# Gates spread by DMA with a later multiply, and the MLPs' inner chunks in groups of four

## The chip, the cores and the metric

The kernel runs on one core of a Trainium2 chip. A core has engines with an instruction stream of their own: TensorE (PE, matrix products), VectorE (DVE), ScalarE (ACT, among other things exp and gelu, whose tables it loads), GpSimd (POOL) and SyncE (SP, which issues most of the transfers here). Each works through its stream in order and waits for others by semaphores. Products land in PSUM, which has eight banks of 128 x 512 floats. The metric is the device time of one execution in microseconds.

## The reference

32 sequences ("batches" below) of 128 tokens with 144 channels pass through four layers, each conditioned by a vector per sequence:

```python
x = _L0_cond_ref(x, ...)  # attention with normed q and k, then gelu(h @ w1 + b1) @ w2 + b2
x = _L1_cond_ref(x, ...)  # a rotation by expm(A) in a subspace of 64
x = _L2_cond_ref(x, ...)  # attention (16 heads of 9), then an MLP with 576 inner channels
x = _L3_cond_ref(x, ...)  # attention, then a mixture of 4 experts, 576 inner channels each
```

In L3 each token weighs its two best experts. Every expert is computed for every token, and multiplied by the token's gate `cw`, which is zero for the two that were not chosen:

```python
cw = jnp.sum(one_hot(topk_idx, NUM_EXPERTS) * gates[..., None], axis=1)
hmid = gelu(einsum('tc,ech->eth', xf, w1) + b1[:, None, :])
eo = einsum('eth,ehc->etc', hmid, w2) + b2[:, None, :]
moe = einsum('te,etc->tc', cw, eo)
```

## The kernel before

**Blocks, groups, ticks.** The kernel treats L0 (with L1 behind it), L2 and L3 as three blocks, `layer` 0, 1, 2 in the code; "second block" is L2 and "third block" is L3. The 32 batches of a block go in eight groups of G = 4. Time is laid out by hand in *ticks*: each tick starts the attention of one batch and works on two older ones, and is cut into named *gaps* in a fixed order: a, e, t, first half of the scores, stats, the weighing of values, o, b0, b, den, pre1, second half of the scores, c, y1, y2, y3, then the row maxima are transposed (nm, L870), z, d, and the attention's projection (L1013) ends the tick. `put(tick, gap, f, ...)` hangs a piece of work in a gap; `put2(tick, gap, to, f, ...)` hangs its first half in one gap and its second in another. Group n of a block starts at tick `t0 = first[layer] + 4 n`, its q and k are made at t0 − 2 and its MLP from t0 + 8 on. The order of calls is the order of each engine's stream: nothing reorders it later.

**PSUM.** `bank` (L82-87) hands out seven of the banks in turn, `ps_m`. A product that takes the next bank waits until the one who used that bank seven takings before has been read out.

**Contraction of 144.** Inputs are kept transposed, 128 channels as the *main* part (hM) and the other 16 with a one for the bias as the *rest* (hR), which stands four times, on each of four tiles of 32 rows (it gets there through a DRAM round trip, hG to hD to hR, L709 and L712). `both` (L717-725) issues the main products of some chunks of 128 outputs and then their rest products, or the other way (`rest_first`), adding up in the same bank. Rest products on different row tiles can run side by side. One fp32 product leaves two rows in the profile.

**q and k.** `qk_chunks` (L753-781) makes q and k of a whole group: three chunks with rests on row tiles 0, 1 and 2, then four ScalarE instructions read the three banks (L766, L774 to L776).

**The MLP of the second block.** 576 inner channels are five chunks of 128, the last half full and called SHARED (index 8 in `hid`). `fc1` (L1020-1038) makes some chunks for all four batches of a group, N = 512, then a small gelu that brings in the table (L1034) and the gelus from PSUM into `hid` (L1037). The rest of chunk m lies on row tile m modulo 3. The group's chunks 0, 1, 2 are made at t0 + 8, and 3 and SHARED at t0 + 9, in gap c, rests first. `mlp2` (through `fc2`, L1040-1044) makes the second layer for one batch: five products into one bank, the last with SHARED. It stands in gaps b and d of t0 + 10 and b and c of t0 + 11.

**The experts of the third block.** The experts are computed in pairs. A pair has nine chunks: four full ones per expert, and one, SHARED, whose halves are the last 64 channels of both. `moe1` (L1166-1168) makes them in three parts of three chunks (part 1 begins with SHARED) at t0 + 8 for pair 0 and t0 + 10 for pair 1, parts 0 and 1, and part 2 one tick later. `moe2_parts` (L1186-1202) makes the second layer of one expert for one batch: four products, which VectorE scales by the gate into `acc`, and, for the pair's even expert, one more product from SHARED, which VectorE adds as it is. For this SHARED must have the gates in it already: `shared_by_gate` (L1171-1180) has POOL spread the pair's gates over 64 columns each (`cwx`), PE transpose the four batches' 128 x 128 (`ps_cw`) and VectorE multiply `hid[:, SHARED]` by the result in PSUM, in gap y1 of the tick that makes SHARED.

Of the kernel before, what the change touches and what calls it, by code (L numbers as in the profile page):

```python
# [12 lines left out]
ALU = mybir.AluOpType  # L13
# [12 lines left out]
SHARED = 8  # L26
NPC = 9
MLP_COLS = NFC * (128 + 128 + C)
PAIR_COLS = NPC * (256 + C)
# [40 lines left out]
def tile_kernel(ctx: ExitStack, tc: tile.TileContext, a: dict, out: bass.AP):  # L70
# [182 lines left out]

    take_nm = ring([128, 128], "nm", 2, fill_nm)
    take_kT = ring([128, 4, G * T], "kT", 2, lambda t: None)
    take_qk = ring([128, 32, SLOT], "qkn", 2, fill_qk)
# [489 lines left out]
    def qk_tiles(g):  # L746
# [4 lines left out]
        return gr[g]["qT"], gr[g]["kT"]  # L751

    def qk_chunks(g):  # L753


        p = PARAMS[g[0]]
        hM, hR = gr[g]["hM_a"], gr[g]["hR_a"]
        qT, kT = qk_tiles(g)
        pss = [bank([128, G * T], f"ps_qk_{g[0]}_{g[1]}_{m}") for m in range(3)]
        cols = [slice(128 * m, 128 * m + 128) for m in range(3)]  # L760
        yield from both(
            [(ps, p.wqk[:, c], hM) for ps, c in zip(pss, cols)],
            [(ps, p.wqkR[rows4(m), cols[m]], hR[rows4(m)]) for m, ps in enumerate(pss)],
            False,
        )
        nc.scalar.copy(qT[:, 0, :], pss[0])  # L766
        if g[0] == 1 and g[1] < 2:
            nc.gpsimd.tensor_copy(kT[:, 3, :], kmask[:, 3:4].to_broadcast([128, G * T]))
        if g == (1, 0):
            for r in (1, 2):  # L770
                nc.scalar.mul(kT[:, r, :], pss[1], kmask[:, r : r + 1])
            gr[g]["k"] = kT, pss[1]
        else:
            nc.scalar.mul(kT[:, 2, :], pss[1], kmask[:, 2:3])  # L774
            nc.scalar.copy(kT[:, 1, :], pss[1])  # L775
        nc.scalar.copy(qT[:, 1, :], pss[2])  # L776
        for j in range(4):
            r = 32 * j + 1
            nc.sync.dma_start(
                kT[r : r + HD, 3, :], qT[r + PITCH : r + PITCH + HD, 1, :]  # L780
            )
# [237 lines left out]

    def fc1(g, p, name, m, to, rest_first):  # L1020


        hM, hR = gr[g]["hM_m"], gr[g]["hR_m"]
        pss = [bank([128, G, T], f"ps_h_{name}_{m + i}") for i in range(len(to))]
        cols = [slice(128 * (m + i), 128 * (m + i) + 128) for i in range(len(to))]
        tiles = [rows4((m + i) % 3) for i in range(len(to))]
        yield from both(
            [(ps, p.w1[:, c], hM) for ps, c in zip(pss, cols)],
            [(ps, p.w1R[r, c], hR[r]) for ps, c, r in zip(pss, cols, tiles)],
            rest_first,  # L1030
        )

        t = small.tile([128, 1], F32, tag="gelu", name=f"gelu_{name}_{m}", bufs=1)
        nc.scalar.activation(t, half, AF.Gelu_apprx_tanh)  # L1034
        for ps, i in zip(pss, to):
            n = 64 if g[0] < 2 and i == SHARED else 128
            nc.scalar.activation(hid[:n, i], ps[:n], AF.Gelu_apprx_tanh)  # L1037
# [8 lines left out]
    def mlp1(g, m, to, rest_first):  # L1046
        return fc1(g, MLPS[g[0]], f"{g[0]}_{g[1]}", m, to, rest_first)

# [65 lines left out]
    def expert_ranks(g):  # L1114


        lg = gr[g]["lg"]
        sh = [128, G, E]
        sh4 = [128, G, E, E]
        cw = small.tile(sh, F32, tag="cw", name=f"cw_{g[1]}", bufs=2)  # L1120
# [45 lines left out]
    def moe1(g, pair, part, rest_first):  # L1166
        to = ((0, 1, 2), (SHARED, 3, 4), (5, 6, 7))[part]
        return fc1(g, PAIRS[pair], f"3_{g[1]}_{pair}", 3 * part, to, rest_first)

    def shared_by_gate(g, pair):  # L1170


        cwx = late.tile([128, G, 2, 64], F32, tag="cwx", name=f"cwx_{g[1]}_{pair}", bufs=1)
        cw = gr[g]["cw"][:, :, 2 * pair : 2 * pair + 2]
        nc.gpsimd.tensor_copy(cwx, cw.unsqueeze(3).to_broadcast([128, G, 2, 64]))
        yield
        ps = bank([128, G, T], f"ps_cw_{g[1]}_{pair}")
        for i in range(G):
            nc.tensor.transpose(ps[:, i, :], cwx[:, i, :, :].rearrange("p e c -> p (e c)"), ident)  # L1179
        nc.vector.tensor_tensor(hid[:, SHARED], hid[:, SHARED], ps, ALU.mult)  # L1180

# [4 lines left out]
    def moe2_parts(g, e, i):  # L1186
# [7 lines left out]
        yield  # L1194
        if e % 2 == 0:
            nc.tensor.matmul(  # L1196
# [3 lines left out]
        nc.vector.scalar_tensor_tensor(acc, ps[:, 0, :], w, acc, ALU.mult, ALU.add)  # L1200
        if e % 2 == 0:
            nc.vector.tensor_tensor(acc, acc, ps[:, 1, :], ALU.add)
# [123 lines left out]
    for layer in range(3):  # L1326
        ahead = 5 if layer == 0 else 6
        for n in range(NG):
# [344 lines left out]
```

## Time and profile before

| what | us |
|---|---|
| median of 3 runs (lowest, highest) | 1279.36 (1277.12, 1282.75) |
| the profiled execution's own time | 1276.88 |
| its span, first to last instruction | 1275.2 |
| PE busy | 1226.3 (96% of the span) |
| DVE busy | 808.1 (63%) |
| ACT busy | 779.4 (61%) |
| POOL busy | 667.9 (52%) |
| inner products of all MLPs, ps_h from hM (L721) | 144.1 for the group of tile mlps |
| table loads for gelu (L1034) | 58 of 1.283 |
| table loads for exp (L934) | 57 of 1.283 |
| transposes of spread gates (L1179) | 64 instructions |

The mean granted clock of PE is 0.989 of full speed. In the trace the second block's attention runs from about 420 us and the third's from about 800 us; the first 420 us hold the first block, the rotation's preparation and loads of weights. A row of a time line gives the start, the time from the start of the first to the end of the last instruction in it, engine, line, operation and tiles, and how many; in brackets stands idle time just before it and who ended it. An engine's starts tell the pitch of its instructions better than their durations, since PE overlaps them.

### The profile page before, as it was taken

The page shows a single profiled execution, that of the slowest core. Times are in us where ns is not written, and L with a number is a line of the kernel's source. Part 1 is how long each engine was busy: PE and PEld are TensorE (multiplying, and loading weights), DVE is VectorE, ACT ScalarE, POOL GpSimd, SP SyncE. Part 2 cuts the span into 40 slices and gives each one's busy share as a digit, 9 for nine tenths or more (in the row PEclk, how much of TensorE's full clock was granted, in tenths as well). Part 3 has the DMA queues.
Part 4 walks back from the last instruction along what each step waited for, and adds up shares of the span by engine and source line. Part 5 has one row for each costly group of instructions (what it writes and reads, how often), then busy time and mean ns, then how long its engine had stood idle before and what let it go on. Part 6 is the DMA issues. An engine that isn't in the chain of part 4 may idle for free.

```text
span 1275.2 us, 35382 instructions
## 1 busy us (share of the span) xinstructions
PE 1226.3 (96%) x13980; PEld 898.6 (70%) x13980; DVE 808.1 (63%) x2540; ACT 779.4 (61%) x1724; POOL 667.9 (52%) x1641
## 2 busy tenths in 40 slices
PE   6889888999989999999999999999999999999998
PEld 4668666778766677767677777767676767677666
DVE  5598888877875466666666766645454646454343
ACT  2467777688776665667666666565656555555431
POOL 5567777766754444444545554626262636261610
PEclk9699999999999999999999999999999999999999
DMA  8301011010013111111121111210101010100000
GB/s 227 75 4 38 3 37 37 2 38 21 20 36 132 56 39 55 35 49 45 41 87 56 56 47 46 85 47 15 51 11 55 11 55 11 55 20 17 20 27 10
DMA packets 50328, 56.49 MB, mean 44 GB/s; under 512 B 4560, under 2 KB 35792, under 8 KB 49904
## 3 DMA queue, kind: packets, MB, share of 16 engines
q1 hardware_dynamic: 49504, 53.75, 14.2%
q8 instruction: 113, 1.85, 0.6%
q10 hardware_dynamic: 656, 0.44, 0.2%
q14 instruction: 55, 0.45, 0.1%
HBM read 39.99 MB, written 13.00 MB: 42 GB/s over the span
## 4 chain that ended last, share of the span: by engine, by line
PE 70%; DVE 4%; ACT 0%; issue 0%; POOL 0%; DVEq 0%
PE ps_h L721 20%; PE ps_f L1191 10%; PE ps_s L918 7%; PE ps_w L918 6%; PE ps_o L949 6%; PE ps_qk L721 5%; PE ps_f L1043 4%; PE ps_pj L1013 3%; PE ps_v L721 3%; PE ps_f L1196 1%; DVE nm L930 1%; PE ps_o L870 1%; PE ps_hT_m L690 1%; PE ps_cw L1179 1%; PE ps_hT_a L690 1%; PE ps_d L1092 0%
## 5 line engine op out<-in xcount | busy, mean ns | idle before, releaser
L930 DVE TENSOR_REDUCE nm<-ps_s 128x4 f32<-128x512 f32 x384 | 246.5, 683 | 95.9 <-PE ps_w L918 74.8
L934 ACT ACTIVATE pr<-ps_w 128x512 f32<-128x512 f32 x384 | 208.5, 595 | 149.7 <-PE ps_w L918 141.0
L918 PE MATMUL ps_s<-kT,qT 32*128 32x256 f32 (+2 forms) x1536 | 235.1, 409 | 0.9 <-ACT kT L850 0.9
L918 PE MATMUL ps_w<-q,kT 32*128 32x128 f32 x3072 | 230.0, 284 | 0.0
L918 PEld LDWEIGHTS ps_w<-q,kT 32*128 32x128 f32 x3072 | 194.4, 187 | 11.0 <-issue 6.2
L1037 ACT ACTIVATE hid<-ps_h 128x512 f32<-128x512 f32 (+1 forms) x224 | 120.4, 590 | 99.8 <-PE ps_h L721 99.4
L918 PEld LDWEIGHTS ps_s<-kT,qT 32*128 32x128 f32 x1536 | 136.9, 187 | 29.4 <-issue 9.2
L721 PE MATMUL ps_h<-hM_m,mlps 128*128 128x512 f32 x304 | 144.1, 607 | 0.0
L1200 DVE SCALAR_TENSOR_TENSOR acc<-ps_f,cw,acc 128x144 f32<-128x144 f32 x128 | 46.7, 365 | 146.3 <-PE ps_f L1191 71.5
L999 POOL TENSOR_TENSOR x_sb<-x_sb,res_a 128x144 f32<-128x144 f32 x96 | 46.9, 489 | 156.5 <-DVE res_a L1002 155.8
L949 PE MATMUL ps_o<-pr,vaug 128*32 128x128 f32 x3072 | 104.4, 277 | 0.0
L949 PEld LDWEIGHTS ps_o<-pr,vaug 128*32 128x32 f32 x3072 | 78.6, 110 | 32.7 <-PE ps_w L918 17.4
L721 PEld LDWEIGHTS ps_h<-hM_m,mlps 128*128 128x128 f32 x304 | 53.4, 190 | 66.9 <-issue 65.6
L1043 PE MATMUL ps_f<-mlps,hid 128*128 128x144 f32 x640 | 93.7, 294 | 0.0
L1043 PEld LDWEIGHTS ps_f<-mlps,hid 128*128 128x128 f32 x640 | 82.4, 191 | 8.8 <-issue 4.7
L934 ACT ACT_TABLE_LOAD x57 | 73.1, 1283 | 10.0 <-PE ps_w L918 9.1
L793 POOL TENSOR_SCALAR kT<-kT,cst 128x512 f32<-128x512 f32 x30 | 46.9, 1562 | 58.5 <-ACT kT L775 57.0
L1034 ACT ACT_TABLE_LOAD x58 | 74.4, 1283 | 1.0
L661 POOL TENSOR_SCALAR rs_m_a<-mv_m_a 128x2 f32<-128x2 f32 x81 | 15.5, 191 | 113.5 <-DVE mv_m_a L659 86.6
L1191 PEld LDWEIGHTS ps_f<-pair,hid 128*128 128x128 f32 x512 | 66.9, 190 | 8.4 <-issue 7.6
L701 ACT ACTIVATE hM_m<-ps_hT_m,modM 128x128 f32<-128x128 f32 x96 | 44.6, 465 | 45.8 <-PE ps_hT_m L690 43.8
L1191 PEld LDWEIGHTS ps_f<-mlps,hid 128*128 128x128 f32 x512 | 66.7, 190 | 7.9 <-issue 6.9
(336 smaller groups left out, 2756.2 us busy)
## 6 DMA issues: line engine op xcount, KB each, us to landing
gates<-gates SPq DMA_DIRECT2D x48, 288.0 KB
hD_m<-hG_m SPq DMA_DIRECT2D x24, 256.0 KB
hR_m<-hD_m SPq DMA_DIRECT2D x24, 256.0 KB
hD_a<-hG_a SPq DMA_DIRECT2D x16, 256.0 KB
hR_a<-hD_a SPq DMA_DIRECT2D x16, 256.0 KB
x_sb<-in_x SPq DMA_DIRECT2D x8, 288.0 KB
out_x<-x_sb SPq DMA_DIRECT2D x7, 288.0 KB
mlps<-in_L_mlp SPq DMA_DIRECT2D x2, 1000.0 KB
```

What stands on the lines that cost most here:

```text
L721: nc.tensor.matmul(ps, x, y, start=k == 0, stop=k == 1)
L793: eng.tensor_scalar(o, k, m, None, ALU.mult)
L918: nc.tensor.matmul(o, x, y, start=True, stop=True)
L930: nc.vector.tensor_reduce(to, view, AX.X, ALU.max, negate=True)
L934: nc.scalar.activation(pr[:, 4 * e : 4 * e + 4, :].rearrange("p s q -> p (s q)"), view, AF.Exp, scale=SCALE,)
L949: nc.tensor.matmul(po[rows4(j), t, :], v[:, 4 * j + 2 * t + r, :], prs[j // 2][:, 4 * (j % 2) + 2 * r + t, :], start=r == 0, stop=r == 1,)
L999: nc.gpsimd.tensor_tensor(x_sb[:, b, :], x_sb[:, b, :], t, ALU.add)
L1034: nc.scalar.activation(t, half, AF.Gelu_apprx_tanh)
L1037: nc.scalar.activation(hid[:n, i], ps[:n], AF.Gelu_apprx_tanh)
L1043: nc.tensor.matmul(ps, hid[:, at0, i, :], w2[:, m, :], start=m == 0, stop=m == NFC - 1)
L1191: nc.tensor.matmul(ps[:, 0, :], hid[:, at0 + m, i, :], w2[:, at0 + m, :], start=m == 0, stop=m == 3)
L1200: nc.vector.scalar_tensor_tensor(acc, ps[:, 0, :], w, acc, ALU.mult, ALU.add)
```

## The change

It has three parts.

1. **Second block.** A group's chunks 0 to 3 are made together at t0 + 8 in gap c, main rows first, with rests on row tiles 0 to 3. The fifth, SHARED, is made with the q and k of the group three later (or of the third block's first groups), at t0 + 10 in gap c, as a fourth chunk of `qk_chunks` with its rest on row tile 3; its gelu comes after the four ScalarE instructions of q and k. `mlp2` of the four batches stands in d of t0 + 10 and b, c and d of t0 + 11.
2. **Third block, pair 1 of groups 0 to 4.** Chunks 0, 1, 2 and 4 at t0 + 10 and 5 to 8 at t0 + 11, rests first, and SHARED (chunk 3) with the q and k of the group three later at t0 + 10. Pair 0 of all groups and pair 1 of groups 5 to 7 keep their three parts.
3. **Gates.** The gates are kept as rows e, i of one 128 x 128 tile (`cwz`); one transpose per group turns it, ScalarE copies 16 rows, one transfer writes them to DRAM, and per pair two transfers spread them over 64 partitions each (`gate_rows`, `gate_rows_of`). VectorE multiplies SHARED by that tile in SBUF a tick later than before, in gap stats. One buffer serves both pairs. The SHARED product of batch 0 of a group moves from the pair's even expert to its odd one.

The packing of the rest weights follows the tiles (`MLP_TILES`).

```diff
+MLP_TILES = {
+    "L0": (0, 1, 2, 0, 1), "L2": (0, 1, 2, 3, 3),
+    "L3_0": (0, 1, 2, 0, 1, 2, 0, 1, 2), "L3_1": (1, 2, 3, 3, 0, 1, 0, 2, 3),
+}
+    take_cw = ring([128, 128], "cwz", 2, zeros)
...
+    JOIN = {(1, n): (1, n - 3) for n in range(3, NG)}
+    JOIN.update({(2, n): (1, n + NG - 3) for n in range(3)})
+    JOIN.update({(2, n): (2, n - 3) for n in range(3, NG)})
...
-        yield from both(
-            [(ps, p.wqk[:, c], hM) for ps, c in zip(pss, cols)],
-            [(ps, p.wqkR[rows4(m), cols[m]], hR[rows4(m)]) for m, ps in enumerate(pss)],
-            False,
-        )
+        main = [(ps, p.wqk[:, c], hM) for ps, c in zip(pss, cols)]
+        rest = [(ps, p.wqkR[rows4(m), cols[m]], hR[rows4(m)]) for m, ps in enumerate(pss)]
+        f = JOIN.get(g)
+        if f is not None:
+            l, mlp, m = ("L2", MLPS[1], 4) if f[0] == 1 else ("L3_1", PAIRS[1], 3)
+            psh, main_h, rest_h = fc1_products(f, l, mlp, f"{f[0]}_{f[1]}_s", (m,))
+            main, rest = main + main_h, rest + rest_h
+        yield from both(main, rest, False)
...
         nc.scalar.copy(qT[:, 1, :], pss[2])
+        if f is not None:
+            gelus(f, f"{f[0]}_{f[1]}_s", psh, m, (SHARED,))
...
-    def fc1(g, p, name, m, to, rest_first):
+    def fc1_products(g, l, p, name, ms):
...
+    def fc1(g, l, p, name, ms, to, rest_first):
+        pss, main, rest = fc1_products(g, l, p, name, ms)
+        yield from both(main, rest, rest_first)
+        gelus(g, name, pss, ms[0], to)
...
-        to = ((0, 1, 2), (SHARED, 3, 4), (5, 6, 7))[part]
-        return fc1(g, PAIRS[pair], f"3_{g[1]}_{pair}", 3 * part, to, rest_first)
+        ms = range(3 * part, 3 * part + 3)
+        if part > 2:
+            ms = ((0, 1, 2, 4), (5, 6, 7, 8))[part - 3]
+        to = [(0, 1, 2, SHARED, 3, 4, 5, 6, 7)[m] for m in ms]
+        return fc1(g, f"L3_{pair}", PAIRS[pair], f"3_{g[1]}_{pair}", ms, to, rest_first)
...
-        cwx = late.tile([128, G, 2, 64], F32, tag="cwx", name=f"cwx_{g[1]}_{pair}", bufs=1)
-        cw = gr[g]["cw"][:, :, 2 * pair : 2 * pair + 2]
-        nc.gpsimd.tensor_copy(cwx, cw.unsqueeze(3).to_broadcast([128, G, 2, 64]))
-        yield
-        ps = bank([128, G, T], f"ps_cw_{g[1]}_{pair}")
-        for i in range(G):
-            nc.tensor.transpose(ps[:, i, :], cwx[:, i, :, :].rearrange("p e c -> p (e c)"), ident)
-        nc.vector.tensor_tensor(hid[:, SHARED], hid[:, SHARED], ps, ALU.mult)
+        ws = gr[g]["cwb"].rearrange("p (i t) -> p i t", i=G)
+        nc.vector.tensor_tensor(hid[:, SHARED], hid[:, SHARED], ws, ALU.mult)
+
+    def gate_rows(g):
+        ps = bank([128, 128], f"ps_cw_{g[1]}")
+        nc.tensor.transpose(ps, gr[g]["cwz"], ident)
+        rows = late.tile([128, T], F32, tag="lgT", name=f"cwT_{g[1]}")[: E * G]
+        nc.scalar.copy(rows, ps[: E * G])
+        gr[g]["cwD"] = dram.tile([E * G * T], F32, name=f"cwD_{g[1]}")
+        nc.sync.dma_start(gr[g]["cwD"].rearrange("(r t) -> r t", t=T), rows)
+        gate_rows_of(g, 0)
+
+    def gate_rows_of(g, pair):
+        ws = gr[g]["cwb"] = late.tile([128, G * T], F32, tag="cwb", name=f"cwb_{g[1]}_{pair}")
+        for e in range(2):
+            at0 = (2 * pair + e) * G * T
+            nc.sync.dma_start(
+                ws[64 * e : 64 * e + 64], gr[g]["cwD"][at0 : at0 + G * T].partition_broadcast(64)
+            )
...
-        if e % 2 == 0:
+        shared = e % 2 == (i == 0)
+        if shared:
...
-                put2(t0 + 8, "c", "c", mlp1, g, 0, (0, 1, 2), True)
-                put2(t0 + 9, "c", "c", mlp1, g, 3, (3, SHARED), True)
+                put2(t0 + 8, "c", "c", mlp1, g, 0, (0, 1, 2, 3), False)
                 for i in range(G):
-                    put(t0 + (10, 10, 11, 11)[i], "bdbc"[i], mlp2, g, i)
+                    put(t0 + (10, 11, 11, 11)[i], "dbcd"[i], mlp2, g, i)
...
+                put(t0 + 8, "den", gate_rows, g)
+                put(t0 + 9, "den", gate_rows_of, g, 1)
...
-                    put2(at_, "stats", "b0", moe1, g, pair, 0, True)
+                    if pair and n < NG - 3:
+                        put2(at_, "stats", "b0", moe1, g, pair, 3, True)
+                        put2(at_ + 1, "stats", "b0", moe1, g, pair, 4, True)
+                    else:
+                        put2(at_, "stats", "b0", moe1, g, pair, 0, True)
...
-                    else:
+                    elif not pair or n >= NG - 3:
                         put2(at_, "den", "pre1", moe1, g, pair, 1, False)
-                    put2(at_ + 1, "stats", "b0", moe1, g, pair, 2, True)
-                    put2(at_, "stats", "y1", shared_by_gate, g, pair)
+                    if not pair or n >= NG - 3:
+                        put2(at_ + 1, "stats", "b0", moe1, g, pair, 2, True)
+                    put(at_ + 1, "stats", shared_by_gate, g, pair)
```

More of the change, by code (lines that the diff above doesn't have):

```diff
@@ L1018, in project_sum, with gelus @@
         residual(b, st[s].pop("pj"), gr[g]["ga"][:, i, :], f"a_{s}", layer == 0)
-    def fc1(g, p, name, m, to, rest_first):
+    def fc1_products(g, l, p, name, ms):
         hM, hR = gr[g]["hM_m"], gr[g]["hR_m"]
[L1024 to L1031, printed above, removed]
+        pss = [bank([128, G, T], f"ps_h_{name}_{m}") for m in ms]
+        cols = [slice(128 * m, 128 * m + 128) for m in ms]
+        tiles = [rows4(MLP_TILES[l][m]) for m in ms]
+        main = [(ps, p.w1[:, c], hM) for ps, c in zip(pss, cols)]
+        rest = [(ps, p.w1R[r, c], hR[r]) for ps, c, r in zip(pss, cols, tiles)]
+        return pss, main, rest
+    def fc1(g, l, p, name, ms, to, rest_first):
+        pss, main, rest = fc1_products(g, l, p, name, ms)
+        yield from both(main, rest, rest_first)
+        gelus(g, name, pss, ms[0], to)
+    def gelus(g, name, pss, m, to):
         t = small.tile([128, 1], F32, tag="gelu", name=f"gelu_{name}_{m}", bufs=1)
@@ L1046, in mlp1 @@
     def mlp1(g, m, to, rest_first):
-        return fc1(g, MLPS[g[0]], f"{g[0]}_{g[1]}", m, to, rest_first)
+        ms = range(m, m + len(to))
+        return fc1(g, ("L0", "L2")[g[0]], MLPS[g[0]], f"{g[0]}_{g[1]}", ms, to, rest_first)
     def mlp2(g, i):
@@ L1119, in expert_ranks @@
         sh4 = [128, G, E, E]
-        cw = small.tile(sh, F32, tag="cw", name=f"cw_{g[1]}", bufs=2)
+        gr[g]["cwz"] = take_cw()
+        cw = gr[g]["cwz"][:, : E * G].rearrange("p (e i) -> p i e", i=G)
         rank = small.tile(sh, F32, tag="rank", name=f"rank_{g[1]}", bufs=2)
@@ L1200, in moe2_parts @@
         nc.vector.scalar_tensor_tensor(acc, ps[:, 0, :], w, acc, ALU.mult, ALU.add)
-        if e % 2 == 0:
+        if shared:
             nc.vector.tensor_tensor(acc, acc, ps[:, 1, :], ALU.add)
@@ L1592, with mlp @@
         arrays[f"{name}_wproj"] = wp
-    def mlp(name, w1, b1, w2):
+    def mlp(name, w1, b1, w2, tiles):
         rest = np.zeros((128, w1.shape[1]), w1.dtype)
         for m in range(w1.shape[1] // 128):
-            k, cols = m % 3, slice(128 * m, 128 * m + 128)
+            k, cols = tiles[m], slice(128 * m, 128 * m + 128)
             rest[32 * k : 32 * k + CR, cols] = w1[CM:, cols]
@@ L1609 @@
         w2 = np.vstack([w2, b2, pad[:63, :1].repeat(C, 1)])
-        mlp(l, np.hstack([w1, pad[:C]]), np.hstack([b1, pad[C]]), w2)
+        mlp(l, np.hstack([w1, pad[:C]]), np.hstack([b1, pad[C]]), w2, MLP_TILES[l])
     for n in range(2):
@@ L1619 @@
         w2 = np.vstack([w2[0][:512], w2[1][:512], w2[0][512:], w2[1][512:]])
-        mlp(f"L3_{n}", w1, b1, w2)
+        mlp(f"L3_{n}", w1, b1, w2, MLP_TILES[f"L3_{n}"])
     arrays["L3_b2"] = inputs["L3_cond_b2"].ravel()
```

## The prediction

> **What bounds the kernel now.** I read the busy time by stage first, since the page's averages mix three blocks. The last five stages cover blocks two and three:
>
> ```profile
> 420.00:570.00 150.00, 149.36 (x1739) 106.56 (x1738) 96.86 (x279) 94.33 (x185) 71.30 (x162) 1.00 0.17 49
> 570.00:800.00 230.00, 227.78 (x2842) 165.28 (x2844) 155.09 (x440) 151.07 (x292) 117.64 (x246) 1.00 0.19 56
> 800.00:1000.00 200.00, 199.96 (x1927) 140.93 (x1919) 107.18 (x330) 115.42 (x214) 96.63 (x207) 1.00 0.12 39
> 1000.00:1180.00 180.00, 179.60 (x1768) 129.94 (x1769) 93.60 (x277) 101.54 (x183) 80.64 (x175) 1.00 0.10 30
> 1180.00:1275.00 95.00, 90.18 (x579) 61.57 (x571) 36.76 (x111) 33.14 (x66) 28.75 (x59) 1.00 0.07 19
> ```
>
> Columns: stretch, length, busy PE, PEld, DVE, ACT, POOL, clock, DMA share, GB/s. PE is busy 757 of 760 us up to 1180 at clock 1.00. Work taken from PE shortens the kernel one to one; a hole in PE's stream lengthens it by as much, unless a later wait shrinks with it, and hardly a wait is left.
>
> Second, the time line of PE where q and k of a group are made, and ScalarE's of the same stretch:
>
> ```profile
> 606.18 2.84 PE L721 MATMUL ps_qk<-hM_a,L_wqk 128*128 128x512 f32 x6
> 608.95 1.13 PE L721 MATMUL ps_qk<-hR_a,L_wqkR 32*128 32x512 f32 x6
> 610.01 0.33 PE L870 MATMUL ps_o<-cst,nm 128*128 128x128 f32 x1
> 610.18 1.39 PE L1043 MATMUL ps_f<-mlps,hid 128*128 128x144 f32 x10
> 611.40 0.27 PE L690 MATMUL ps_hT_m<-cst,xh_m 128*128 128x128 f32 x1
> ```
>
> ```profile
> 610.11 0.58 ACT L766 COPY qT<-ps_qk 128x512 f32<-128x512 f32 x1 [2.64 <-PE ps_qk L721]
> 610.59 0.69 ACT L774 ACTIVATE kT<-ps_qk,cst 128x512 f32<-128x512 f32 x1
> 611.17 0.59 ACT L775 COPY kT<-ps_qk 128x512 f32<-128x512 f32 x1
> 611.63 0.61 ACT L776 COPY qT<-ps_qk 128x512 f32<-128x512 f32 x1
> ```
>
> Three chunks' rest rows cost 610.01 − 608.95 = 1.06 us beside 2.77 of main rows, and a second-layer product follows at a pitch of 1.22/10 = 0.122. ScalarE empties the q and k banks until 612.24, which is 2.23 after the rests end.
>
> Third, ScalarE at an inner layer, the price of a gelu from a cold table:
>
> ```profile
> 587.77 1.28 ACT L1034 ACT_TABLE_LOAD   x1
> 589.07 0.20 ACT L1034 ACTIVATE gelu<-half 128x1 f32<-128x1 f32 x1
> 589.18 1.69 ACT L1037 ACTIVATE hid<-ps_h 128x512 f32<-128x512 f32 x3
> ```
>
> The first real gelu starts 1.41 after its table load and takes 0.59 (mean in the page's groups: 0.590).
>
> **The change, part by part.**
>
> *Slots saved.* Chunks of a rest slot run side by side on 32-row tiles; a fourth tile is free beside three. Block two has 5 chunks in two slots, and gets one own slot (four chunks) and a place in q and k's slot: 8 slots fewer. In block three pair 1 of groups 0 to 4 goes from three slots to two and a place: 5 fewer. 13 × 1.06 = −13.8 us on PE, booked below with the block that each belongs to. That four tiles run together shows in the scores: at 605.07 and 605.09 eight rows of scores on four tiles start as one. [...]
>
> *Gates.* Per pair four transposes go (908.73 to 909.22: 0.49), per group one (0.11) comes. Pair 0: 8 × (0.11 − 0.49) = −3.0. Pair 1 of the three groups that keep their form: −1.5; that of the other five is inside the next part. POOL loses 16 copies, which nobody on PE waited for, and the shared product of a pair's first batch moves to its second expert, 0.24 here or there. New: one ScalarE copy of 128x128 per group (0.45 like hM's), and 40 transfers on SP's queue. The gate rows leave after out_x (872.95, held by POOL), and the multiply is wanted by PE at the shared product, 884.77 in that group. The nearest row for a trip through DRAM:
>
> ```profile
> 872.95 0.39 SPq L1211 DMA_DIRECT2D out_x<-x_sb  x1
> 891.28 0.37 SPq L709 DMA_DIRECT2D hD_a<-hG_a  x1
> 894.99 0.33 SPq L712 DMA_DIRECT2D hR_a<-hD_a  x1
> ```
>
> 3.7 us for the way out, as much for the way back: 873.35 + 3.7 + 0.7 for two issues + 3.7 = 881.5, then 0.68 of multiply: 2.6 us to spare; the queue has nothing behind them until 891.28. The second pair's broadcasts wait on the queue for the first multiply (one buffer), which DVE, idle 881.3 to 885.2, gives in time. Taken: 0, and +1 for the last group, where PE has less other work; bounds −0.5 and +3 per group.
>
> *The joined chunk of block two.* Its gelu stands on ScalarE behind the four copies of q and k, and needs the table. With T the end of the rests: copies to T+2.23, table and start +1.41, gelu +0.59: T+4.2. But fc2 of the group's first batch now stands at "d" of this very tick, behind the maxima's transpose: its fifth product reads that chunk, and PE is there at T + 0.17 + 8 × 0.122 = T+1.15. PE is in order, so everything of the tick behind it (transposes of h, pj, the next scores) waits 3.1 us. Eight groups: +24.8. Bounds: 2.6, if the table were loaded half a microsecond sooner, and 3.6 with a mask or transfer in the way of a copy.
>
> *The group of four in block two.* Before, rests came first and each gelu followed its own main product (589.18 while PE ran to 590.07). Now mains come first, so no bank is whole until the rests run. With the table loaded by then, four gelus follow at a pitch of 0.48 (three take 1.55 at 897.56): banks free at T+0.69, 1.17, 1.65 and 2.13. Seven banks turn in a ring. Counted out from the order of PE, the next tick's first scores get the banks of the third and fourth gelu in groups 0 to 5, and PE wants them at T+1.35 (the maxima, transposes and projection lie between): 2.13 − 1.35 = 0.75 to 0.8 of waiting. In groups 6 and 7 the values' products lie between too: 0.3. 4 × 0.75 + 2 × 0.8 + 2 × 0.3 = +5.2. Bounds: 0 and 8 × 1. The other fc2 products only change places within two ticks; they cost the same.
>
> *Pair 1 of five groups in block three.* Rest rows first, so a fourth bank is taken before the scores' banks are read out:
>
> ```profile
> 892.67 0.59 PE L918 MATMUL ps_s<-kT,qT 32*128 32x384 f32 x2
> 893.64 1.06 PE L721 MATMUL ps_h<-hR_m,mlps 32*128 32x512 f32 x6
> ```
>
> ```profile
> 893.83 1.29 DVE L930 TENSOR_REDUCE nm<-ps_s 128x4 f32<-128x512 f32 x2 [0.69 <-PE ps_w L918]
> ```
>
> The fourth rest row waits for the first reduce, 893.83 + 0.69 = 894.52 against 893.64: +0.9. The other four-chunk slot likewise: +0.85. After q and k the next scores take the bank that the joined gelu frees at T+4.2, wanted at T+2: +2.2. Together 3.95, less about 0.4 because each hole gives DVE time for the next. Against it stand the group's saved slot, 1.06, and its transposes, 0.49: 3.95 − 0.4 − 1.55 = +2.0. Five groups: +10. Bounds: −1.55 each (no wait comes) and +3. Ten more table loads of 1.28 lie in this on ScalarE, which is busy 115 of 200 us.
>
> *Sum.* Block two: 24.8 + 5.2 − 8 × 1.06 = +21.5. Block three: +10 − 3.0 − 1.5 + 1 = +6.5. Together +28 on the profiled execution's 1276.88 us, which lies 2.5 under the median of the runs (1279.36): about 1305.
>
> [...]
>
> **The rivals.**
> - *Everything arrives in time* (the other side: faster). −13.8 − 7.0 (64 transposes less 8) = −21: 1256. It needs the joined gelu within T+1.15 in block two; half way to this is where the stall falls under 1.1 us, as then 8 × 1.06 pays for it. For it: ScalarE is idle half its time. Against it: its own order, copies ahead of the gelu, and 1.41 of table.
> - *Only the stall in block two*: all the bank waits hidden by other waits. 24.8 − 13.8 − 7.0 = +4: 1281.
> - *Gates late*: transfers of 128 KB slower than those above by 3 us past their slack. DVE then holds the multiply and behind it the sums' reads, and PE the shared product: 3 × 8 = 24 more: 1329. Against it: DMA share 0.10 to 0.12 here.
> - *The fourth tile does not run beside three*: each four-tile slot 0.86 longer, like a main chunk (2.77/3 = 0.92 at most). Of 31 such slots (16 in block two, 15 in block three) those before a wait hide it; 13 do not: +11, 1316. Against it: the scores' rows.
>
> **How the numbers follow.** The sum 0.65, in 1290 to 1318; all in time 0.10; only the stall 0.10; gates late 0.08; fourth tile 0.07. Predicted 1305. The range 1280 to 1322 leaves out the first rival, the gates' and the tails: 0.2. What a measurement tells from no change is about 0.5%, 6.4 us: faster 0.10, same 0.09 (most of the second rival), slower 0.81.
>
> **What the profile of the changed kernel would show.** Right: at ps_f behind ps_qk in block two a hole on PE of about 3 us ended by the gelu, eight times; holes of under 1 us at the scores behind the group of four, ended by ScalarE; in block three holes at ps_h's rests ended by DVE and at scores ended by ScalarE; PE's share some 2% lower; ps_cw at 8 transposes. Rest slots of eight rows at about 1.1 us. Wrong: the gelu of the joined chunk before the copies, a hole ended by a DMA at the shared product, or a clock under 1.00 after holes, which no row here prices.

## The result: 70 us slower, more than twice the loss that was forecast

The changed kernel takes 1351.18 us (median of 6 runs, 1345.42 to 1357.08) against 1281.03 us for the kernel before (6 runs, 1277.12 to 1284.04). The ratio is 1.0555, its 95% interval 1.0516 to 1.0593. The forecast was 1305, range 1280 to 1322: the direction was right and the size was not. The profiled execution has a span of 1351.4 us.

The stages of the second and third block in the profile after (columns as before: stretch, length, busy PE, PEld, DVE, ACT, POOL, clock, DMA share, GB/s):

```profile
420.00:570.00 150.00, 144.53 (x1602) 103.32 (x1603) 88.17 (x256) 86.72 (x170) 66.84 (x150) 0.97 0.15 44
570.00:800.00 230.00, 202.09 (x2384) 147.37 (x2378) 131.94 (x372) 127.66 (x243) 97.64 (x206) 0.94 0.15 47
800.00:1000.00 200.00, 187.66 (x1891) 133.26 (x1888) 104.75 (x316) 118.31 (x217) 90.34 (x187) 0.97 0.15 48
1000.00:1180.00 180.00, 176.55 (x1606) 122.03 (x1604) 89.33 (x262) 104.08 (x184) 84.52 (x174) 0.96 0.12 39
1180.00:1351.00 171.00, 164.68 (x1313) 115.69 (x1313) 77.09 (x230) 76.74 (x145) 55.00 (x117) 1.00 0.11 32
```

Two columns have changed: PE now has idle time in every stage, and the clock, which was 1.00 in all five, lies between 0.94 and 1.00. Both must be read. For all kernels of this study I split PE's time from 420 us to its last instruction into three: idle time between its rows, half of the time it worked at a granted clock of one half (what that cost), and the rest. The rest is the work at full clock; waits too short to show as a gap between two rows are still in it. All three are worked out from PE's rows and the clock's rows of the profiled executions, to about half a microsecond; a gap counts as idle from 0.15 us.

| kernel (profiled execution, us) | rest | idle | lost to half clock |
|---|---|---|---|
| before | 847.1 | 3.5 | 0 |
| after | 846.9 | 50.3 | 29.3 |

Idle time adds 46.8 and the half clock 29.3, together 76.1, which is what the span grew by (1351.4 − 1275.2 = 76.2). The rest is level, though 56 transposes and 13 slots were removed, some 18 us by the rows (an estimate: 7 and 11). As much was lost again inside rows that the profile calls busy; the places are named below.

Whom PE waited for (engine, line and tile that waited, who ended the wait: us in total, times, the longest), profile after:

```profile
PE ps_f L1060 <- ACT hid L1054: 23.7, 8, 3.0
PE ps_o L884 <- DVE nm L944: 18.9, 15, 2.6
...
PE ps_w L932 <- ACT hid L1054: 4.4, 4, 1.1
PE ps_f L1230 <- DVE hid L1196: 1.9, 1, 1.9
```

The first line is the forecast wait for the joined gelu. The second was not forecast. Before, this wait came to 2.3 us in five places:

```profile
PE ps_o L870 <- DVE nm L930: 2.3, 5, 0.7
```

**The joined gelu.** The tick that makes q, k and the fifth chunk, PE first, then ScalarE:

```profile
582.81 0.33 PE L884 MATMUL ps_o<-cst,nm 128*128 128x128 f32 x1
582.98 1.15 PE L1060 MATMUL ps_f<-mlps,hid 128*128 128x144 f32 x8
587.09 0.85 PE L1060 MATMUL ps_f<-mlps,hid 128*128 128x144 f32 x2 [2.96 <-ACT hid L1054]
...
588.15 1.17 PE L1027 MATMUL ps_pj<-L_wproj,oT 128*128 128x144 f32 x4
```

```profile
584.43 0.61 ACT L788 COPY qT<-ps_qk 128x512 f32<-128x512 f32 x1
585.06 1.28 ACT L1051 ACT_TABLE_LOAD   x1
586.35 0.20 ACT L1051 ACTIVATE gelu_s<-half 128x1 f32<-128x1 f32 x1
586.46 0.57 ACT L1054 ACTIVATE hid<-ps_h_s 64x512 f32<-64x512 f32 x1
```

Eight products of the four chunks that were ready, then a hole of 2.96 until the gelu behind the last copy and the table load is done. The hole has the same length in all eight groups.

**The clock.** Behind this hole the projection's four products take 1.17 us from first start to last end, against 0.66 in the profile before:

```profile
590.83 0.66 PE L1013 MATMUL ps_pj<-L_wproj,oT 128*128 128x144 f32 x4
```

The same stretch of the profile after, in windows of 2 us, shows why:

```profile
584.00:586.00 2.00, 0.13 (x2) 0.00 (x0) 0.00 (x0) 1.98 (x4) 0.00 (x0) 1.00 0.00 0
586.00:588.00 2.00, 0.91 (x4) 0.91 (x5) 0.03 (x1) 1.02 (x3) 0.00 (x0) 0.52 0.08 18
588.00:590.00 2.00, 2.00 (x14) 1.72 (x16) 0.59 (x2) 0.81 (x2) 0.74 (x2) 0.50 0.08 18
...
594.00:596.00 2.00, 2.00 (x32) 1.70 (x31) 1.35 (x4) 0.76 (x3) 1.89 (x5) 1.00 0.22 74
```

The clock falls to one half from 586.1 and comes back at 592.9. Eleven such stretches, of 3.41 or 6.83 us, lie between 420 us and the end of PE's work; the kernel before has none there (the half clock in its first 420 us and behind PE's last row is not counted).

**The maxima.** The tick behind the group of four, where the second slot used to stand, PE's last scores and what follows, then VectorE:

```profile
571.17 0.28 PE L932 MATMUL ps_w<-q,kT 32*128 32x128 f32 x2
572.93 0.30 PE L884 MATMUL ps_o<-cst,nm 128*128 128x128 f32 x1 [1.48 <-DVE nm L944]
```

```profile
571.50 1.28 DVE L944 TENSOR_REDUCE nm<-ps_s 128x4 f32<-128x512 f32 x2
```

PE wants to transpose the row maxima of the scores, and VectorE has only just begun to reduce the second half of them. Before, a slot of two chunks stood at t0 + 9 between the scores and this transpose, 2.78 us (596.60 to 599.38) in which the reduces ran unseen:

```profile
596.60 1.02 PE L721 MATMUL ps_h<-hR_m,mlps 32*128 32x512 f32 x4
597.56 1.99 PE L721 MATMUL ps_h<-hM_m,mlps 128*128 128x512 f32 x4
599.38 0.27 PE L870 MATMUL ps_o<-cst,nm 128*128 128x128 f32 x1
```

The change emptied that place. The hole is 1.48 in groups 0 to 3 and 2.1 to 2.6 in groups 4 to 7.

### The profile page after: what moved, and what is told of

It is laid out like the page before. It is cut to its first block, busy times and chain, and to the rows that moved or that the text cites. A ratio compares the mean times of both kernels' runs of the same rounds, so it can differ in the third digit from the quotient of the medians.

```text
span 1351.4 us, 35333 instructions
## 1 busy us (share of the span) xinstructions
PE 1254.7 (93%) x13924; PEld 915.5 (68%) x13924; DVE 810.5 (60%) x2540; ACT 797.6 (59%) x1742; POOL 667.8 (49%) x1627
## 4 chain that ended last, share of the span: by engine, by line
PE 62%; DVE 6%; ACT 5%; issue 2%; DMA 1%; POOL 0%; SPq 0%; DVEq 0%; ACTq 0%
PE ps_h L726 18%; PE ps_f L1224 8%; PE ps_s L932 6%; PE ps_w L932 6%; PE ps_o L963 5%; PE ps_qk L726 4%; PE ps_f L1060 3%; PE ps_pj L1027 3%; DVE nm L944 2%; PE ps_v L726 2%; ACT L1051 1%; PE ps_f L1230 1%; PE ps_h_s L726 1%; PE ps_o L884 1%; ACT pr L948 1%
## 5 line engine op out<-in xcount | busy, mean ns | idle before, releaser
L932 PE MATMUL ps_w<-q,kT 32*128 32x128 f32 x3072 | 241.5, 291 | 4.4 <-ACT hid L1054 4.4
L932 PE MATMUL ps_s<-kT,qT 32*128 32x256 f32 (+2 forms) x1536 | 241.9, 419 | 0.9 <-ACT kT L864 0.9
L932 PEld LDWEIGHTS ps_w<-q,kT 32*128 32x128 f32 x3072 | 202.7, 193 | 14.6 <-ACT hid L1054 8.2
L932 PEld LDWEIGHTS ps_s<-kT,qT 32*128 32x128 f32 x1536 | 142.0, 192 | 32.7 <-issue 13.2
L1054 ACT ACTIVATE hid<-ps_h 128x512 f32<-128x512 f32 (+1 forms) x211 | 113.7, 594 | 84.8 <-PE ps_h L726 84.7
L1234 DVE SCALAR_TENSOR_TENSOR acc<-ps_f,cwz,acc 128x144 f32<-128x144 f32 x128 | 46.8, 365 | 186.5 <-PE ps_f L1224 97.6
L726 PE MATMUL ps_h<-hM_m,mlps 128*128 128x512 f32 x278 | 132.8, 616 | 0.0
L1060 PE MATMUL ps_f<-mlps,hid 128*128 128x144 f32 x640 | 96.1, 295 | 23.7 <-ACT hid L1054 23.7
L963 PE MATMUL ps_o<-pr,vaug 128*32 128x128 f32 x3072 | 111.1, 288 | 0.0
L963 PEld LDWEIGHTS ps_o<-pr,vaug 128*32 128x32 f32 x3072 | 83.2, 115 | 36.4 <-issue 16.2
L948 ACT ACT_TABLE_LOAD x62 | 79.5, 1283 | 19.7 <-PE ps_w L932 18.9
L1013 POOL TENSOR_TENSOR x_sb<-x_sb,res_m 128x144 f32<-128x144 f32 x64 | 32.8, 514 | 93.8 <-DVE res_m L1016 93.8
```

The lines of the kernel that those rows point to most:

```text
L726: nc.tensor.matmul(ps, x, y, start=k == 0, stop=k == 1)
L932: nc.tensor.matmul(o, x, y, start=True, stop=True)
L948: nc.scalar.activation(pr[:, 4 * e : 4 * e + 4, :].rearrange("p s q -> p (s q)"), view, AF.Exp, scale=SCALE,)
L963: nc.tensor.matmul(po[rows4(j), t, :], v[:, 4 * j + 2 * t + r, :], prs[j // 2][:, 4 * (j % 2) + 2 * r + t, :], start=r == 0, stop=r == 1,)
L1013: nc.gpsimd.tensor_tensor(x_sb[:, b, :], x_sb[:, b, :], t, ALU.add)
L1060: nc.tensor.matmul(ps, hid[:, at0, i, :], w2[:, m, :], start=m == 0, stop=m == NFC - 1)
```

## The experiments

Times are medians. The first four share 13 runs of the kernel before (1277.79), the next four 7 runs (1278.92), the last four 19 (1278.93). The split of each profiled execution:

| kernel | median | ratio to before (95%) | rest | idle | half clock |
|---|---|---|---|---|---|
| gates | 1275.09 | 0.9981 (0.9954 to 1.0009) | 842.9 | 5.2 | 0 |
| l2g | 1331.09 | 1.0411 (1.0385 to 1.0438) | 845.7 | 45.5 | 11.5 |
| l3g | 1295.58 | 1.0112 (1.0075 to 1.0149) | 851.9 | 10.4 | 10.2 |
| fc2_late | 1328.77 | 1.0392 (1.0365 to 1.0418) | 860.9 | 28.9 | 11.9 |
| gelu_first | 1303.43 | 1.0203 (1.0158 to 1.0248) | 843.4 | 22.0 | 8.5 |
| cover | 1306.77 | 1.0202 (1.0155 to 1.0249) | 863.7 | 16.6 | 1.7 |
| cover_rests | 1311.29 | 1.0252 (1.0206 to 1.0299) | 855.9 | 21.6 | 5.1 |
| cover_rests_l2 | 1305.5 | 1.0185 (1.0131 to 1.0239) | 851.9 | 21.8 | 8.3 |
| filler | 1297.1 | 1.0149 (1.0113 to 1.0185) | 866.1 | 7.6 | 0 |
| three_one | 1278.46 | 1.0000 (0.9976 to 1.0024) | 844.9 | 8.8 | 0 |
| three_one_l3 | 1285.14 | 1.0035 (1.0009 to 1.0060) | 848.6 | 8.7 | 1.7 |
| four_rests | 1328.62 | 1.0403 (1.0366 to 1.0441) | 839.0 | 31.1 | 31.5 |

The theory to test was: the loss is holes on PE that the moved chunks open, and the half clock follows from the holes. The rivals: the half clock comes from something else that is new (four-tile slots, transfers), the loss lies mainly in the third block, or the gates' transfers cost.

### The three parts, one by one

`gates` keeps both blocks' chunks as before and has the new gates alone:

```diff
-    JOIN = {(1, n): (1, n - 3) for n in range(3, NG)}
-    JOIN.update({(2, n): (1, n + NG - 3) for n in range(3)})
-    JOIN.update({(2, n): (2, n - 3) for n in range(3, NG)})
+    JOIN = {}
...
-                    if pair and n < NG - 3:
+                    if pair and (2, n + 3) in JOIN:
...
-                put2(t0 + 8, "c", "c", mlp1, g, 0, (0, 1, 2, 3), False)
+                put2(t0 + 8, "c", "c", mlp1, g, 0, (0, 1, 2), True)
+                put2(t0 + 9, "c", "c", mlp1, g, 3, (3, SHARED), True)
                 for i in range(G):
-                    put(t0 + (10, 11, 11, 11)[i], "dbcd"[i], mlp2, g, i)
+                    put(t0 + (10, 10, 11, 11)[i], "bdbc"[i], mlp2, g, i)
```

> Part 3 of the change alone: gates spread by DMA and multiplied a tick later, both blocks' inner chunks as before. Theory (holes on PE and the half clock after them, all from the chunks): 56 transposes fewer, -7 us, and the one wait of 1.9 us at the last group's shared product, so -5: 1276. No half clock beyond the first 420 us. Rival (the transfers and the later multiply hold up the third block): +5 or more: 1286 and waits for a DMA or for hid at ps_f.

`l2g` adds the second block's part to that (its JOIN holds the first two lines), `l3g` the third block's (its JOIN holds {(2, n): (2, n − 3)} alone, and the second block is placed as in `gates`).

> Parts 1 and 3: the second block's chunks as in the change, the third block's pair 1 in three parts as before. Theory: in the second block 8 holes of 2.96 at ps_f (24), 8 at the row maxima (17), some 5 behind the group of four, 18 of half clock, less 7 for the slots: +57, with the gates' -5: 1333. Rival (the third block's joined groups carry most of the loss): below 1310.

> Parts 2 and 3: the second block as before, the third block's pair 1 as in the change. Theory: 5 holes of about 1 after q and k, some 6 of waiting inside the rest rows, 10 of half clock in three places, less 4 for the slots: +16, with the gates' -5: 1292. Rival (the half clock is brought over from the second block's holes and does not arise here): +6 - 5: 1282.

Measured: 1275.09, 1331.09 and 1295.58. Against `gates`, the second block's part costs 56.0 us and the third's 20.5; with the 2.7 that the gates alone lie under before, that makes 73.8, beside the 70.2 measured for the whole. The second block carries the loss, so that rival falls. The gates' transfers do harm in one place alone: at the last group VectorE waits 2.5 us for the spread gates, and PE behind it 2.0 us for the multiplied SHARED:

```profile
DVE hid L1194 <- DMA cwb<-cwD: 2.5, 1, 2.5
```

```profile
PE ps_f L1228 <- DVE hid L1194: 2.0, 1, 2.0
```

In `gates` there is no half clock between 420 us and PE's last row, and its time is not told apart from before. In `l3g` the half clock arises in the third block with no hole in the second, so it is not brought over:

```profile
800.00:1000.00 200.00, 195.97 (x1800) 133.88 (x1796) 99.44 (x300) 119.24 (x213) 94.51 (x198) 0.97 0.15 51
1000.00:1180.00 180.00, 177.91 (x1675) 126.33 (x1668) 94.69 (x285) 101.90 (x184) 81.97 (x172) 0.98 0.11 36
```

### Taking the reader of the late gelu away

```diff
-                    put(t0 + (10, 11, 11, 11)[i], "dbcd"[i], mlp2, g, i)
+                    put(t0 + 11, "bbcd"[i], mlp2, g, i)
```

> The change with one edit: in the second block the four fc2 products of a group all stand at t0 + 11 (b, b, c, d), so none waits for the joined chunk's gelu in its own tick. Theory (the holes are the cause, and the half clock follows from them): the eight holes of 2.96 go, 24, and the half clock behind them, about 11: 1351 - 35 = 1316; the holes at the row maxima stay. Rival (the half clock comes from the four-tile rest slots or the transfers, not from the holes): -24 alone: 1327, with as many stretches at half clock as before. Second rival (the wait moves to the next reader of that bank or to ScalarE's exps): above 1340.

1328.77: 22 less than after, where 35 was expected. The eight holes at ps_f are gone, and the half clock fell from 29.3 to 11.9, but the rest grew by 14. The time line of the same tick shows where the rest grew: the scores of the next tick, whose bank the late gelu still holds, run from 580.79 to the weighing at 583.17, 2.4 us where such scores take 1.1 (595.35 to 596.45 in the same trace). Two of their lines:

```profile
580.79 0.91 PE L932 MATMUL ps_s<-kT,qT 32*128 32x384 f32 x4
581.60 1.08 PE L932 MATMUL ps_w<-q,kT 32*128 32x128 f32 x7
```

So the wait moved in part to the next reader of the bank, inside rows that the profile calls busy. Eight times 1.2 explains 10 of the 14. The second rival was right in kind, not in size. That the first rival had named 1327 is chance: it wanted as many stretches of half clock as before, and they fell from eleven to six.

### The gelu ahead of the copies

The table is loaded before the products, and the gelu is issued before q's and k's four instructions:

```diff
             main, rest = main + main_h, rest + rest_h
+            gelu_table(f"{f[0]}_{f[1]}_s", m)
         yield from both(main, rest, False)
+        if f is not None:
+            gelus(f, f"{f[0]}_{f[1]}_s", psh, m, (SHARED,), False)
         nc.scalar.copy(qT[:, 0, :], pss[0])
...
         nc.scalar.copy(qT[:, 1, :], pss[2])
-        if f is not None:
-            gelus(f, f"{f[0]}_{f[1]}_s", psh, m, (SHARED,))
```

> The change with one edit: where a chunk is joined to q and k, gelu's table is loaded before the products, and the gelu stands ahead of the four ScalarE instructions of q and k. Theory (the holes at ps_f come from the place of that gelu behind the copies and a cold table): the gelu is done about 0.7 after the rests, before PE reaches the fifth product at 1.15, so the eight holes of 2.96 (24) go, and the five of about 1 in the third block (5), with their half clock (some 15 to 20); the eight holes at the row maxima stay (19): 1300 to 1308. Rival (ScalarE is late anyway, or the copies of q and k, now 0.5 later, make the next scores wait): 1320 or more. If the gelus are in time and the clock still drops as often: 1322.

1303.43, as expected: 47.8 less than after for one move. ScalarE and PE in that tick now:

```profile
569.29 1.28 ACT L1052 ACT_TABLE_LOAD   x1
570.59 0.20 ACT L1052 ACTIVATE gelu_s<-half 128x1 f32<-128x1 f32 x1
572.82 0.59 ACT L1059 ACTIVATE hid<-ps_h_s 64x512 f32<-64x512 f32 x1 [2.03 <-PE ps_h_s L726]
```

```profile
572.85 1.39 PE L1065 MATMUL ps_f<-mlps,hid 128*128 128x144 f32 x10
```

The ten products run through. The holes of the third block behind q and k are gone too, and the copies, half a microsecond later, cost nothing that shows. Of the 22.0 us of idle time that are left, 19.5 are at the maxima.

### What the emptied gap cost

`cover` moves the group of four to t0 + 9 and puts one fc2 into gap c of t0 + 12, so that no gap c is empty. `cover_rests` makes the rests first as well, and `cover_rests_l2` takes the third block's join out of that.

```diff
-                put2(t0 + 8, "c", "c", mlp1, g, 0, (0, 1, 2, 3), False)
+                put2(t0 + 9, "c", "c", mlp1, g, 0, (0, 1, 2, 3), False)
                 for i in range(G):
-                    put(t0 + (10, 11, 11, 11)[i], "dbcd"[i], mlp2, g, i)
+                    put(t0 + 11 + (i == 3 and n < NG - 1), ("bcdc" if n < NG - 1 else "bcdd")[i], mlp2, g, i)
```

> As gelu_first, and the second block's group of four moves from t0 + 8 to t0 + 9, with one fc2 (1.2 us) put into gap c of the following tick 0, so that no tick of four has an empty gap c between the second half of the scores and the transpose of the row maxima. Theory (the holes of 1.5 to 2.6 at the row maxima arise because the removed chunks stood between the scores and the maxima's transpose and covered VectorE's reduces): 17 of 19 us of these holes go and the half clock behind them: 1280 to 1288. Rival (VectorE is late for another reason): as gelu_first.

> As cover, with the rest rows of the second block's group of four first. Theory (main rows first keep all four banks until the end, and the next scores wait 0.75 us for the gelus): some 4 to 6 us less than cover. Rival (rests first make the fourth bank wait for the scores' reduces instead, as in the third block): no gain, or a loss of up to 7.

> As cover_rests, with the third block's pair 1 in three parts as before (no join there). Theory (with the joined gelu in time the third block's join still loses: about 6 of waiting inside the rest rows against 4 for the slots): 2 to 4 less than cover_rests, so about 1270 to 1276, level with or a little under the gates alone. Rival (the third block's only loss was the late gelu): 4 more than cover_rests.

1306.77, 1311.29 and 1305.5: misses, all three. `cover` came out where its rival had put it, near `gelu_first`, and `cover_rests` with the loss that its own rival allowed. Idle time fell by only 5 us in `cover`, and the rest grew by 20. Moving the group had changed two things at once: the gap was filled with 1.2 us, which covers a part only (holes of about 0.5 and 1.05 remain), and the four banks of the group now meet the four of the joined products in the next tick (what this costs was not measured by itself). The runs could not tell the cover from the banks, so the next one fills the gap and moves nothing. `filler` is `gelu_first` with two products whose result nobody reads:

```diff
                 put2(t0 + 8, "c", "c", mlp1, g, 0, (0, 1, 2, 3), False)
+                put(t0 + 9, "c", filler, g)
```

> As gelu_first, with two useless main products (128x512, 0.9 us each, their result read by nobody) in the empty gap c of the second block's tick t0 + 9, eight times: 14.4 us more work for PE. Theory (the holes at the row maxima are there because nothing stands between the scores and the maxima's transpose): the products fill the holes, four of 1.55 and four of 2.2 to 2.7, so about 13 of idle time and 4 to 7 of half clock behind the longer ones go: 1294 to 1304, no slower than gelu_first (1303). Rival (VectorE is late because its own work starts late): +14, 1317.

1297.1, as expected: the 32 useless rows keep PE busy for 15.9 us, and still the kernel is 6.3 us faster than `gelu_first`; each of its four runs lies under each of the other's four, if narrowly (1300.35 against 1300.43). The waits of PE at the maxima in `gelu_first` and then in `filler`:

```profile
PE ps_o L885 <- DVE nm L945: 19.5, 18, 2.7
```

```profile
PE ps_o L885 <- DVE nm L945: 5.6, 14, 0.8
```

And the stage in which most of the second block lies, in `gelu_first` and then in `filler`:

```profile
570.00:800.00 230.00, 215.00 (x2618) 158.63 (x2616) 143.13 (x406) 141.84 (x271) 107.46 (x226) 0.97 0.17 48
```

```profile
570.00:800.00 230.00, 226.17 (x2712) 161.75 (x2710) 147.66 (x421) 144.71 (x276) 108.95 (x230) 1.00 0.17 51
```

VectorE's work did not change (809.9 us busy in the one profile, 809.4 in the other); its lateness shows only when PE has nothing else to do. Filling the holes also took the four half-clock stretches behind them away (the five of `gelu_first` cost 8.5 us, and `filler` loses 0). So here it was the holes that brought the half clock: chunks, four-tile slots and transfers all stayed. The fifth stretch of `gelu_first`, at 1266, is no witness for this: it follows the last group's wait for the gates (1.87), which `filler` still has (1.77), there without half clock behind it. Of the rest, which is 22.7 larger than in `gelu_first`, some 7 are not accounted for by the useless rows.

### Group of four, or three and one

`four_rests` is `gelu_first` with the group's rest rows first:

```diff
-                put2(t0 + 8, "c", "c", mlp1, g, 0, (0, 1, 2, 3), False)
+                put2(t0 + 8, "c", "c", mlp1, g, 0, (0, 1, 2, 3), True)
```

> As gelu_first, with the rest rows of the second block's group of four first instead of last. Theory (main first leaves four banks to four gelus that come only at the end, 0.75 at the next scores): the wait behind the group goes, 5, but the fourth rest row now waits for the scores' reduce, 0.9 each, 7: within 4 of gelu_first's 1303. Rival A (only the bank wait behind it counts): 1298. Rival B (both waits): 1310.

1328.62, worse than either rival: 25 more than `gelu_first`. PE's waits:

```profile
PE ps_o L885 <- DVE nm L945: 20.1, 17, 2.7
...
PE ps_h L726 <- DVE nm L945: 8.4, 8, 1.4
```

One of these slots:

```profile
549.83 1.06 PE L726 MATMUL ps_h<-hR_m,mlps 32*128 32x512 f32 x6
551.81 1.12 PE L726 MATMUL ps_h<-hR_m,mlps 32*128 32x512 f32 x2 [0.91 <-DVE nm L945]
552.86 4.54 PE L726 MATMUL ps_h<-hM_m,mlps 128*128 128x512 f32 x6
```

The fourth tile's two rows wait for VectorE's reduces, 1.05 us on average, and then run alone for another 1.05 (551.81 to 552.86) instead of beside the other three: 3.03 in all, where the eight together take 1.07. The half clock rises from 8.5 to 31.5. These 23.0 are most of the 27.7 by which the two profiled spans differ; the idle time grew by 9.1, and the rest fell by 4.4.

`three_one` leaves chunk 3 alone at t0 + 9, where it covers the reduces, keeps the join with the gelu first, and has the third block's pair 1 as before; `three_one_l3` joins there as well.

```diff
-                put2(t0 + 8, "c", "c", mlp1, g, 0, (0, 1, 2, 3), False)
+                put2(t0 + 8, "c", "c", mlp1, g, 0, (0, 1, 2), True)
+                put2(t0 + 9, "c", "c", mlp1, g, 3, (3,), True)
```

> Gates by DMA; second block: chunks 0 to 2 at t0 + 8 as before, chunk 3 alone at t0 + 9 (rests first, 1.4 us of cover), the fifth joined to q and k with its gelu ahead of the copies; third block's pair 1 as before. Theory (lost cover and banks held by four gelus make what is left of the loss): against the gates alone, rest slots of one tile for two save about 3.6, holes of up to 1.2 at the maxima of the last four groups cost up to 5: 1272 to 1280. Rival (a fourth bank taken by the joined chunk costs by itself): 1290 or more.

> As three_one, with the third block's pair 1 of groups 0 to 4 joined as in the change, its gelu ahead of the copies. Theory: the holes after q and k are gone there, but each four-tile rest slot of rests first still waits some 0.9 for VectorE's reduces: 10 slots, 9 us, against 4 saved: 3 to 6 more than three_one. Rival: 4 less than three_one.

1278.46, as expected, and 1285.14, a little more than expected. Without the group of four the second block's join comes to 3.4 above `gates` (1275.09, in another set of runs), which the runs do not tell apart, as both are level with before; the third block's join costs 6.7 over `three_one` even with its gelu in time. The third block's rest slot, PE and VectorE in `three_one_l3`:

```profile
899.44 2.06 PE L726 MATMUL ps_h<-hR_m,mlps 32*128 32x512 f32 x8
```

```profile
899.63 1.29 DVE L945 TENSOR_REDUCE nm<-ps_s 128x4 f32<-128x512 f32 x2 [0.69 <-PE ps_w L933]
```

Eight rest rows take 1.99 (899.44 to the next product at 901.43) instead of 1.07. The six of the first three tiles start by 899.91, the fourth tile's two at 900.38 and 900.91, when the first of VectorE's two reduces (899.63, 0.69 long) has just ended: they run behind the others, not beside them. That they waited for the bank which this reduce read follows from the order of the banks and these times; no run takes the wait away by itself. The profile calls the whole stretch busy.

No version here beats the kernel before by more than the runs can tell. The gates alone come nearest.

## Why the prediction was wrong, step by step

The steps that failed are two terms which the sum holds at nothing: what the slot at t0 + 9 had covered on VectorE, 16.6 us of new waits at the maxima, and the half clock behind the holes, 29.3 us. Together they are 46 of the 48 us by which the growth of the profiled span, 76.2, passed the +28. One by one:

- **Slots saved, −13.8.** A little too large. A rest slot of one tile takes 0.95 (601.55 to 602.50 in `three_one`), of two 0.95, of three 0.99 to 1.06, and of four 1.07 where nothing holds it up, as here:

```profile
562.50 1.14 PE L726 MATMUL ps_h<-hR_m,mlps 32*128 32x512 f32 x8
563.57 0.33 PE L884 MATMUL ps_o<-cst,nm 128*128 128x128 f32 x1
```

  Per group of the second block 0.99 + 0.95 + 1.07 became 2 × 1.07, a gain of 0.87; 13 of this size make 11 (an estimate: the third block's slots were not priced apart). The fourth tile does run beside three where its bank is free, and the rival that denied it falls as it stands; in the third block's slots, where, by these times, a bank is held, the fourth tile does run behind the others (1.99 in `three_one_l3`). In these rows four tiles take 1.13 times the 0.95 of one.
- **Gates, −7 and +1.** By their pitch the products into ps_cw fell from 16 × 0.49 = 7.8 to 8 × 0.11 = 0.9, as reckoned. The last group's wait was 1.9 instead of 1, and it was one for the transfer; for the other groups the rival of late transfers falls. The gates alone lie 2.7 under before, less than the −6 worked out: in the profiles the rest fell by 4.2 and the idle time grew by 1.7. Why the rest did not fall by 7 was not found.
- **The joined chunk of block two, +24.8.** Right: 8 × 2.96 = 23.7, with the copies, the table and the gelu in the order given.
- **The group of four, +5.2.** Right for the wait that was named, though it does not show as a hole: behind the group of four the scores take 565.00 to 566.90, 0.8 to 0.9 longer than the 1.0 to 1.1 of others, and PE is called busy. But this step looked only at what the four banks hold up, and *Slots saved* only at what the removed slot gives back. Neither asked what the slot at t0 + 9 had covered: VectorE's reduces. This is the first term that is missing from the sum, 16.6 us (18.9 against 2.3 of waits at the maxima).
- **Pair 1 in block three, +10.** Against `gates`, which has the transposes' saving already, this step stands for 5 × (2.0 + 0.49) = 12.5. Measured were 20.5 between the medians and 24.5 between the profiled spans. Of the latter 10.2 are half clock, and the 14 left are near the size given. Inside it the slot's loss was right (2.0 against 1.07), though not as a hole ended by VectorE, as forecast: the rows of the slot run on and only lose their overlap. Behind q and k the hole is 1.09 where 2.2 had been counted; the scores around it take 2.84 (903.57 to 906.41 in the profile after) where 1.1 is usual, so 1.7 in all.
- **The sum, +28.** It put every hole at its own length. The second missing term is the half clock, 29.3. The prediction ended with "a clock under 1.00 after holes, which no row here prices" and then priced it at nothing; the range was not drawn up to it either. While PE works, the kernel before has the clock at half only inside its first 420 us, where PE also waits (a stretch of 20.48 begins in a hole of 5.17, one of 3.41 in a hole of 1.77, another of 3.41 comes 0.9 behind a hole of 0.51), and those rows should have set an upper bound.

With 17 for the maxima and 29 for the clock, the sum would have been +74, and the span grew by 76. That it comes so near is partly luck, as the smaller misses above nearly cancel.

## What to carry to other kernels

Before a piece of work is moved out of a tick, ask what its neighbours did on other engines while it ran: on an engine that is busy all the time, a slot can be someone's cover, and removing it can cost more than it gives back (here 16.6 us of new waits for VectorE against 8 × 0.87 = 7 us of rest rows). Price a hole on TensorE above its own length where the clock has been seen to halve behind such holes: here 50.3 us of idle time came with 29.3 us of half clock. A busy row can hide a wait, above all where rows should run side by side: compare its length with the same row where nothing holds it up (eight rest rows took 1.07, and 1.99 or 3.03 where they waited).

## What was not expected of the hardware

In the profile after, each of the eleven stretches of half clock between 420 us and PE's last row begins in a hole on PE or 0.2 to 2.2 us behind one; five last 3.41 us and six 6.83. The holes of 1 us or more over the same time, and how many had half clock begin in them or in the 2.2 us behind them:

| hole, us | where | holes | with half clock |
|---|---|---|---|
| 2.96 | ps_f behind the joined gelu, second block | 8 | 5 |
| 2.11 to 2.61 | the maxima, groups 4 to 7 | 4 | 2 |
| 1.88 | the last group's multiplied SHARED | 1 | 0 |
| 1.48 | the maxima, groups 0 to 3 | 4 | 1 |
| 1.09 | scores behind q and k, third block | 4 | 3 |

So the length of a hole did not decide by itself: of eight holes of 2.96 three had no half clock behind them, and those of 1.09 had it more often than those of 1.48.

The visible gap is not the whole of it. Around each of the four holes of 1.09 the scores had also lost their running side by side, and take 2.84 where 1.1 is usual, here 903.57 to 906.41:

```profile
903.57 0.76 PE L932 MATMUL ps_s<-kT,qT 32*128 32x384 f32 x2
...
905.75 0.59 PE L932 MATMUL ps_w<-q,kT 32*128 32x128 f32 x5 [1.09 <-ACT hid L1054]
...
906.41 0.59 PE L726 MATMUL ps_h<-hR_m,mlps 32*128 32x512 f32 x1
```

What sets the holes with half clock behind them apart from the others was not shown.
